# A four-layer graph network on one core: inputs and output by partition, adjacency loads in halves, the gates' matmuls spread by chunk

## The chip, the cores and the metric

The kernel runs on one core of one Trainium2 chip, in one launch. The metric is the device time of a run in microseconds (us); the figure quoted for a kernel is the median of its runs, and a ratio compares such times. A separate execution is recorded by the hardware profiler. It has its own time and a span, from its first to its last recorded instruction.

## What is computed

There are 32 independent batches. Each has a feature matrix `x` of 512 x 128 and a dense adjacency matrix `adj` of 512 x 512, all in float32. Four residual layers are applied one after the other, each to a row-normalized and rectified copy of the features:

```python
h = relu(layernorm(x)); x = x + gcn(h, adj)        # L0: normalized by the degree on both sides
h = relu(layernorm(x)); x = x + io_gnn(h, adj)     # L1: adj @ in, adj.T @ out, a node term, tanh
h = relu(layernorm(x)); x = x + unet(h, adj)       # L2: four inner layers with l2-normalized adj
h = relu(layernorm(x)); x = x + gru(h, adj)        # L3: message, then a gated recurrent unit
```

One inner layer of L2 computes `tanh(concat(src_agg, self, dst_agg) @ wu + bu)`, where `src_agg` uses the adjacency normalized along its rows and `dst_agg` the one normalized along its columns. The inner layers take 1, 1, 2 and 3 feature matrices as input, because earlier results are concatenated again. L3 forms `m = tanh(adj @ (h @ W + b))` and then the gates `r`, `z`, `n` from `m` and `h`; the result is `(1 - z) * n + z * h`.

## The kernel before

**Tiling.** The 512 rows of a batch are four chunks (`NC` = 4) of 128 partitions. A feature tile in rows is 128 x 4 x 128, an adjacency tile is 128 x 4 x 512 (1 MB). The kernel holds `adj` as `a` and its transpose as `aT`; `aT` is loaded a second time as `aT2` for L3, since `a` and `aT` are overwritten by their l2-normalized versions (line 602). Weights stay in SBUF; the products of the L2 weights that can be folded are folded once in `setup`. A float32 matmul is seen as two records on TensorE, with a weight load each.

**An operation list and a planner.** `program(b)` does not emit instructions. It records operations for one batch, with an engine, an estimated duration, the buffers read and written and a function that emits the instruction. `Plan.order` (lines 149 to 219) then plays the whole list with these estimates: each engine takes, whenever it is free, the ready operation with the smallest key. The key is a due time, `batch * PERIOD - tail`, where `tail` is the estimated length of the longest chain behind the operation in its batch. The result is one fixed order of instructions for every engine, across all batches. The engines then run these orders strictly in sequence and wait on semaphores. In this way some three batches are in flight at any time: a batch's L1 and its first L2 layers fill TensorE beside the later layers of the batch before it. The planner's durations are estimates (for instance `t_pow`, line 272, for GpSimd's power, and 240 GB/s plus 1.3 us for a DMA, line 99); real durations only shift waits, not the order.

**What a batch does**, with the names that the traces show:

- L0 (lines 498 to 538): `degree` reduces `a` on VectorE (line 503); GpSimd raises variance and degree to the power -0.5 (`sc`, line 404); ScalarE makes `h` from `x` in four instructions (line 416); GpSimd adds the identity to the diagonal blocks of `aT` (`diag`, line 514); TensorE aggregates into `ps_agg`, then `ps_lin`; VectorE makes `z`, `y` and the new features `xr`.
- L1 (lines 541 to 575): normalization again (`bn`, `mv`, `v`, `sc`, `nb`, `h`), a transposition `hT`, two banks of `ps_sd`, `rep`, two aggregations with `aT` and `a`, `ps_upd`, `u`, `y`, `xr`.
- L2 (lines 578 to 634): `inv` is 1/norm of rows and columns, sent through DRAM (`bounce`, `rows`) and multiplied into `aT` and `a` by eight VectorE instructions (line 602). Then, for each of four inner layers, `paired_rows` fills two banks `ps_sd`, VectorE adds a bias to each (`sd`, line 489), and eight matmuls of 512 columns aggregate into `ps_agg`; ScalarE takes the tanh (`f`, line 619). These results are called f1 to f4 below, the transposed input f0.
- L3 (lines 637 to 688): `msg`, the aggregation with `aT2`, `mT` (line 649), and for each of four chunks a bank `ps_gate` with four matmuls: two from `h3T` (128 and 256 columns) and two from `mT` (256 and 128 columns), lines 652 to 660. Then the gate arithmetic `g`, `u`, `q`, `w`, `n`, `xo`, and the store of `out`. For the last two batches (`at_end`) this arithmetic runs by chunk and partly on GpSimd, otherwise on whole tiles.

For the batches 3 to 29 a transposition goes through VectorE (32 x 32 blocks, `blk`, line 425), four DMAs of 64 KB to DRAM (line 434) and one DMA back (line 438); for the others through TensorE (`ps_t`).

**Order of transfers.** All loads and stores except two small ones are issued by SyncE (SP), in one queue order, also taken from the plan. An adjacency load is one DMA of 1 MB (line 378, and line 646 for `aT2`), except for batch 0, which is loaded in four pieces. A DMA that waits for its buffer to come free holds back everything behind it on SP.

The matmuls are all recorded by one helper (line 287):

```python
def mm(ps, out_of, lhs, rhs, n, start, stop, reads, part=None):
    op("PE", t_mm(n), lambda: nc.tensor.matmul(out_of(ps.ap()), lhs(), rhs(), start=start, stop=stop),
       reads, [(ps, part) if part is not None else ps])
```

Of the kernel before, what the change touches and what calls it, by code (L numbers as in the profile page):

```python
# [13 lines left out]
F32 = mybir.dt.float32  # L14
# [66 lines left out]


class Op:
    __slots__ = ("engine", "us", "land", "emit", "after", "next", "waits", "bufs", "batch", "rank", "tail", "ready", "key")


class Plan:
# [28 lines left out]
    def bank(self, name):  # L116
        return self.buf("bank", name=f"ps_{name}")

    def op(self, engine, us, emit, reads=(), writes=(), kb=0.0, rank=None):


        o = Op()
        o.engine, o.us, o.land, o.emit, o.batch, o.rank = engine, us, 0.0, emit, self.batch, rank
        if kb:
            o.us, o.land = max(us, kb / self.RATE), self.TRANSFER
        o.after, o.next, o.bufs = {}, [], []
        for group, written in ((reads, False), (writes, True)):
            for item in group:
                buf, part = item if isinstance(item, tuple) else (item, None)
                if written and buf.old is not None:  # L130
                    for other, _, _ in buf.old.uses:
                        o.after[other] = True
                for other, p, w in buf.uses:
                    if (w or written) and other is not o and (part is None or p is None or part & p):
                        o.after[other] = True
                buf.uses.append((o, part, written))
                if buf not in o.bufs:
                    o.bufs.append(buf)
        self.ops.append(o)
        return o  # L140
# [8 lines left out]
    def order(self):  # L149
        for i, o in enumerate(self.ops):  # L150
            o.waits, o.ready = len(o.after), 0.0
            for other in o.after:
                other.next.append(o)
            for buf in o.bufs:
                buf.left += 1
        for i, o in reversed(list(enumerate(self.ops))):
            o.tail = max([o.us + o.land] + [self.lag(o, n) + n.tail for n in o.next if n.batch == o.batch])

            due = o.batch * PERIOD if o.batch < B - 1 else (B - 2) * PERIOD + ENDING
            o.key = (due - o.tail if o.rank is None else o.rank - 1e6, i)  # L160
        free = {k: list(range(n)) for k, n in self.places.items()}
        unfinished = {}
        for o in self.ops:
            unfinished[o.batch] = unfinished.get(o.batch, 0) + 1
        queues, idle_at = {e: [] for e in self.SIGNAL}, dict.fromkeys(self.SIGNAL, 0.0)
        events, seq = [], 0

        def event(at, what, o=None):
            nonlocal seq
            seq += 1  # L170
            heapq.heappush(events, (at, seq, what, o))

        for o in self.ops:
            if not o.waits:
                event(0.0, "ready", o)
        done = []
        while events:
            now = events[0][0]
            while events and events[0][0] <= now + 1e-9:
                _, _, what, o = heapq.heappop(events)  # L180
                if what == "ready":
                    heapq.heappush(queues[o.engine], (o.key, o))
                elif what == "end":
                    for buf in o.bufs:
                        buf.left -= 1
                        if not buf.left and buf.kind in free:
                            free[buf.kind].append(buf.slot)
                    unfinished[o.batch] -= 1
                    if not unfinished[o.batch]:
                        del unfinished[o.batch]  # L190
            for e, queue in queues.items():
                if idle_at[e] > now + 1e-9:
                    continue
                held, o = [], None
                while queue and o is None:
                    item = heapq.heappop(queue)
                    new = [x for x in item[1].bufs if x.slot is None and x.kind in free]
                    older = item[1].batch - min(unfinished)
                    if any(len(free[x.kind]) < len([y for y in new if y.kind == x.kind]) + older * self.kept.get(x.kind, 0) for x in new):
                        held.append(item)  # L200
                        continue
                    o = item[1]
                    for x in new:
                        x.slot = free[x.kind].pop(0)
                for item in held:
                    heapq.heappush(queue, item)
                if o is None:
                    continue
                done.append(o)
                idle_at[e] = now + o.us  # L210
                event(now + o.us, "idle")
                event(now + o.us + o.land + self.SIGNAL[e], "end", o)
                for n in o.next:
                    n.waits -= 1
                    n.ready = max(n.ready, now + self.lag(o, n))
                    if not n.waits:
                        event(n.ready, "ready", n)
        assert len(done) == len(self.ops), "the plan does not end"
        return done
# [3 lines left out]
def gnn_stack(  # L223
# [60 lines left out]
        ("w1", w_sb), ("w2", w_sb), ("w3", w_sb), ("c_sb", c_sb), ("r_sb", r_sb), ("rf_sb", rf_sb),  # L284
        ("cf_sb", cf_sb), ("ident", ident), ("neg_half", neg_half)))

    def mm(ps, out_of, lhs, rhs, n, start, stop, reads, part=None):
        op("PE", t_mm(n), lambda: nc.tensor.matmul(out_of(ps.ap()), lhs(), rhs(), start=start, stop=stop),  # L288
           reads, [(ps, part) if part is not None else ps])

    def setup():

# [64 lines left out]
    def program(b):  # L357
# [10 lines left out]

        xt, a, aT = buf("s2", rows_shape, "x"), buf("s8", (P, NC, N), "a"), buf("s8", (P, NC, N), "aT")

        pieces = NC if b == 0 else 1

        def load(dst, src, kb, rank):

            n = NC // pieces
            for k in range(pieces):
                s = slice(k * n, (k + 1) * n)
                op("SP", 0.4, lambda s=s: nc.sync.dma_start(dst.ap()[:, s, :], src.rearrange("(c p) n -> p c n", p=P)[:, s, :]),
                   [], [(dst, set(range(NC)[s]))], kb=kb / pieces, rank=None if b else rank)

        op("SP", 0.4, lambda: nc.sync.dma_start(xt.ap(), x[b].rearrange("(c p) d -> p c d", p=P)), [], [xt], kb=256, rank=None if b else 0)
        load(a, adj[b], 1024, 1)
        load(aT, adjt[b], 1024, 4)

# [112 lines left out]

        def degree(v8):
            stat = buf("stat", (P, NC))
            n = NC // pieces  # L500
            for k in range(pieces):
                s = slice(k * n, (k + 1) * n)
                op("DVE", t_tt(n * N), lambda s=s: nc.vector.tensor_reduce(stat.ap()[:, s], a.ap()[:, s, :], AX.X, ALU.add),  # L503
                   [(a, set(range(NC)[s]))], [(stat, {k})])
            op("DVE", 0.08, lambda: nc.vector.tensor_scalar_add(v8.ap()[:, NC:], stat.ap(), 1.0), [stat], [(v8, {1})])
# [7 lines left out]
            blocks = bass.AP(tensor=t.tensor, offset=t.offset + k * (N + P), ap=[list(t.ap[0]), [N + P, n], [1, P]])  # L513
            nc.gpsimd.tensor_tensor(diag.ap()[:, k:k + n, :], blocks, ident[:, None, :].to_broadcast([P, n, P]), op=ALU.add)

        for k in range(0, NC, NC // pieces):
            n = NC // pieces
            op("POOL", t_pool(n * P), lambda k=k, n=n: own(k, n), [(aT, set(range(k, k + n))), ID], [(diag, set(range(k, k + n)))])
        psh = plan.bank("agg")
        for c in range(NC):  # L520
# [122 lines left out]
           N, [psm, (RS, {2})])  # L643
        psa = plan.bank("agg")
        aT2 = buf("s8", (P, NC, N), "aT2")
        op("SP", 0.4, lambda: nc.sync.dma_start(aT2.ap(), adjt[b].rearrange("(c p) n -> p c n", p=P)), [], [aT2], kb=1024)
        aggregate(psa, msg, 0, aT2)
        mT = buf("s2", name="mT")
        op("ACT", t_act(N), lambda: nc.scalar.activation(mT.ap(), psa.ap(), AF.Tanh), [psa], [mT])  # L649
# [2 lines left out]
        for c in range(NC):  # L652
            ps = plan.bank("gate")
            blk = slice(c * P, (c + 1) * P)
            for m, lo, n, col, start, stop in ((h3T, 3, 1, W_L3_HH + 2 * D, True, True), (h3T, 0, 2, W_L3_HH, True, False),
                                               (mT, 0, 2, W_L3_IH, False, True), (mT, 2, 1, W_L3_IH + 2 * D, True, True)):
                mm(ps, lambda t, lo=lo, n=n: t[:, lo * D:(lo + n) * D], lambda m=m, blk=blk: m.ap()[:, blk],
                   lambda col=col, n=n: wt(col, n * D), n * D, start, stop, [m, W3])
            op("DVE", t_tt(N), lambda ps=ps, c=c: nc.vector.tensor_add(g.ap()[:, c, :], ps.ap(), r_sb[:, R_L3_G:R_L3_G + 4 * D]),  # L659
               [ps, RS], [(g, {c})])  # L660

# [10 lines left out]
        for k in range(0, NC, w2):  # L672
            s, part, cols = slice(k, k + w2), set(range(k, k + w2)), w2 * D

            def step(dst, fn, reads, engine="DVE"):
# [8 lines left out]
            step(q, lambda s=s: side.tensor_tensor(q.ap()[:, s, :], q.ap()[:, s, :], x3.ap()[:, s, :], op=ALU.add), [q, x3], side_engine)  # L684
            step(n, lambda s=s: nc.vector.tensor_mul(n.ap()[:, s, :], n.ap()[:, s, :], w.ap()[:, s, :]), [n, w])
            step(xo, lambda s=s: nc.vector.tensor_add(xo.ap()[:, s, :], q.ap()[:, s, :], n.ap()[:, s, :]), [q, n])
            op("SP", 0.4, lambda s=s: nc.sync.dma_start(out[b].rearrange("(c p) d -> p c d", p=P)[:, s, :], xo.ap()[:, s, :]),
               [(xo, part)], [], kb=cols / 2)

    setup()  # L690
# [44 lines left out]
```

## Time and profile before

| quantity | value |
|---|---|
| median of 5 runs | 2386.19 us |
| lowest and highest run | 2384.91 and 2386.62 us |
| the profiled execution's own time | 2385.46 us |
| its span | 2383.5 us |
| TensorE matmul (PE) busy | 2337.3 us, 98% of the span |
| VectorE (DVE) busy | 1297.6 us, 54% |
| ScalarE (ACT) busy | 790.4 us, 33% |
| GpSimd (POOL) busy | 352.0 us, 15% |
| DMA, mean over the span | 82 GB/s |

How to read it: the profiled execution lies 0.73 us below the median of the runs, and 1.96 us of it are outside its span. A busy share is an average; for a chain of dependent work it says little. A timeline row gives the start in the span, the length, the engine, the line, the operation, what it writes and reads, and in brackets how long the engine had been idle before and what ended that. The DMA view gives, for each issue, its size and the time until it has landed. A queue name such as SPq is an engine's sequencer.

### The profile page before, as it was taken

The page shows a single profiled execution, that of the slowest core. Times are in us where ns is not written, and L with a number is a line of the kernel's source. Part 1 is how long each engine was busy: PE and PEld are TensorE (multiplying, and loading weights), DVE is VectorE, ACT ScalarE, POOL GpSimd, SP SyncE. Part 2 cuts the span into 40 slices and gives each one's busy share as a digit, 9 for nine tenths or more (in the row PEclk, how much of TensorE's full clock was granted, in tenths as well). Part 3 has the DMA queues.
Part 4 walks back from the last instruction along what each step waited for, and adds up shares of the span by engine and source line. Part 5 has one row for each costly group of instructions (what it writes and reads, how often), then busy time and mean ns, then how long its engine had stood idle before and what let it go on. Part 6 is the DMA issues. An engine that isn't in the chain of part 4 may idle for free.

```text
span 2383.5 us, 23873 instructions
## 1 busy us (share of the span) xinstructions
PE 2337.3 (98%) x8466; PEld 1427.7 (60%) x8466; DVE 1297.6 (54%) x2963; ACT 790.4 (33%) x1719; POOL 352.0 (15%) x218
## 2 busy tenths in 40 slices
PE   6999999999999999999999999999999999999998
PEld 4565566565666556665556665656655566656655
DVE  6445445565555665555665556654556654554623
ACT  5324223433323333233333234332233322343312
POOL 2101011111011111111110111111111111111001
PEclk9999999999999999999999999999999999999999
DMA  5212122332313222223223132322232232232000
GB/s 216 78 53 68 57 77 83 89 100 86 100 55 102 89 90 96 78 73 104 87 84 107 54 97 89 97 89 85 67 106 89 82 104 63 88 106 71 18 9 9
DMA packets 173206, 196.34 MB, mean 82 GB/s; under 512 B 16800, under 2 KB 105248, under 8 KB 173088
## 3 DMA queue, kind: packets, MB, share of 16 engines
q1 hardware_dynamic: 172800, 194.70, 25.8%
q8 instruction: 66, 1.08, 0.2%
q14 instruction: 52, 0.43, 0.1%
q10 hardware_dynamic: 288, 0.13, 0.0%
HBM read 157.95 MB, written 36.83 MB: 82 GB/s over the span
## 4 chain that ended last, share of the span: by engine, by line
PE 70%; DVE 13%; POOL 7%; ACT 3%; DMA 2%; issue 2%; SPq 1%; POOLq 0%; ACTq 0%; DVEq 0%
PE ps_agg L288 44%; PE ps_sd L288 16%; POOL sc L404 7%; PE ps_gate L288 6%; DVE aT L602 2%; ACT h L416 2%; DVE sd L489 2%; DVE bn L388 2%; DVE a L602 1%; DVE rep L558 1%; PE ps_msg L288 1%; PE ps_lin L288 1%; ACT f L619 1%; DVE node L551 1%; PE ps_upd L288 1%
## 5 line engine op out<-in xcount | busy, mean ns | idle before, releaser
L404 POOL TENSOR_TENSOR sc<-v,neg_half 128x4 f32<-128x4 f32 (+1 forms) x128 | 250.1, 1954 | 1963.6 <-DVE v L391 1908.5
L288 PE MATMUL ps_agg<-aT,sd 128*128 128x512 f32 x1024 | 512.2, 595 | 1.0 <-DVE sd L489 1.0
L288 PE MATMUL ps_agg<-a,sd 128*128 128x512 f32 x1024 | 496.9, 592 | 0.0
L288 PE MATMUL ps_sd<-w_sb,f 128*128 128x256 f32 x1792 | 482.2, 382 | 9.2 <-ACT f L619 8.5
L288 PEld LDWEIGHTS ps_sd<-w_sb,f 128*128 128x128 f32 x1792 | 333.2, 191 | 235.6 <-issue 198.0
L489 DVE TENSOR_TENSOR sd<-ps_sd,rf_sb 128x512 f32<-128x512 f32 x256 | 176.3, 689 | 359.6 <-PE ps_sd L288 357.1
L416 ACT ACTIVATE h<-xr,nb,sc 128x128 f32<-128x128 f32 x384 | 158.0, 482 | 482.9 <-DVE nb L412 482.9
L288 PEld LDWEIGHTS ps_agg<-a,sd 128*128 128x128 f32 x1024 | 185.6, 191 | 164.6 <-issue 155.3
L288 PEld LDWEIGHTS ps_agg<-aT,sd 128*128 128x128 f32 x1024 | 186.9, 190 | 129.0 <-issue 87.7
L288 PE MATMUL ps_agg<-f,w_sb 128*128 128x512 f32 x448 | 229.7, 594 | 0.0
L619 ACT ACTIVATE f<-ps_agg,cf_sb 128x512 f32<-128x512 f32 x128 | 87.2, 681 | 219.9 <-PE ps_agg L288 219.9
L503 DVE TENSOR_REDUCE stat<-a 128x4 f32<-128x2048 f32 (+1 forms) x35 | 73.5, 2102 | 141.0 <-DMA a<-in_adj 141.0
L602 DVE TENSOR_TENSOR a<-a,rows 128x512 f32<-128x512 f32 x128 | 138.5, 1085 | 3.8 <-PE ps_agg L288 3.8
L602 DVE TENSOR_TENSOR aT<-aT,rows 128x512 f32<-128x512 f32 x128 | 137.7, 1081 | 4.5 <-PE ps_agg L288 4.5
L288 PE MATMUL ps_agg<-aT,rep 128*128 128x512 f32 x256 | 130.9, 593 | 2.2 <-DVE rep L558 2.2
L288 PE MATMUL ps_agg<-a,rep 128*128 128x512 f32 x256 | 130.7, 592 | 0.0
L288 PE MATMUL ps_agg<-aT,msg 128*128 128x512 f32 x256 | 125.6, 592 | 0.0
L288 PE MATMUL ps_agg<-aT,h 128*128 128x256 f32 (+2 forms) x384 | 109.9, 383 | 0.0
L412 DVE SCALAR_TENSOR_TENSOR nb<-mv,sc 128x4 f32<-128x4 f32 x128 | 50.8, 397 | 95.4 <-POOL sc L404 95.0
L642 DVE TENSOR_TENSOR msg<-ps_msg,r_sb 128x512 f32<-128x512 f32 x32 | 22.1, 690 | 146.7 <-PE ps_msg L288 146.7
L659 DVE TENSOR_TENSOR g<-ps_gate,r_sb 128x512 f32<-128x512 f32 x128 | 79.5, 683 | 32.1 <-PE ps_agg L288 20.9
L288 PE MATMUL ps_gate<-w_sb,mT 128*128 128x128 f32 (+1 forms) x512 | 94.3, 327 | 0.4 <-ACT mT L649 0.4
(99 smaller groups left out, 2698.5 us busy)
## 6 DMA issues: line engine op xcount, KB each, us to landing
aT<-in_adjt SPq DMA_DIRECT2D x63, 1024.0 KB, 5.6
a<-in_adj SPq DMA_DIRECT2D x31, 1024.0 KB, 5.6
turn_turned<-blk SPq DMA_DIRECT2D x324, 64.0 KB, 1.8
turned<-turn_turned SPq DMA_DIRECT2D x81, 256.0 KB, 2.6
rows<-bounce SPq DMA_DIRECT2D x32, 512.0 KB, 3.8
x<-in_x SPq DMA_DIRECT2D x32, 256.0 KB, 3.0
out<-xo SPq DMA_DIRECT2D x30, 256.0 KB, 2.4
turn_f4r<-blk SPq DMA_DIRECT2D x108, 64.0 KB, 1.9
```

What stands on the lines that cost most here:

```text
L288: op("PE", t_mm(n), lambda: nc.tensor.matmul(out_of(ps.ap()), lhs(), rhs(), start=start, stop=stop), reads, [(ps, part) if part is not Non ...
L388: op("DVE", 0.193, lambda c=c: nc.vector.bn_stats(st.ap()[:, c, :], xin.ap()[:, c, :]), [xin], [(st, {c})])
L404: op("POOL", t_pow(n), lambda: nc.gpsimd.tensor_tensor(inv.ap()[:, :n], v8.ap()[:, :n], neg_half[:, :n], op=ALU.pow), [v8, NH], [(inv, {0})])
L412: op("DVE", 0.08, lambda: nc.vector.scalar_tensor_tensor(nb.ap(), mv.ap()[:, :, 0], -1.0, inv.ap()[:, at:at + NC], op0=ALU.mult, op1=ALU.m ...
L416: op("ACT", t_act(D, 2), lambda c=c: nc.scalar.activation(h.ap()[:, c, :], xin.ap()[:, c, :], AF.Relu, bias=nb.ap()[:, c:c + 1], scale=inv ...
L489: op("DVE", t_tt(N), lambda ps=ps, h=h: nc.vector.tensor_add(sd.ap()[:, 2 * h:2 * h + 2, :], ps.ap().rearrange("p (j v) -> p j v", j=2), a ...
L503: op("DVE", t_tt(n * N), lambda s=s: nc.vector.tensor_reduce(stat.ap()[:, s], a.ap()[:, s, :], AX.X, ALU.add), [(a, set(range(NC)[s]))], [ ...
L551: tt(node, lambda: nc.vector.tensor_max(node.ap(), zn.ap(), en.ap()), N, [zn, en])
L558: op("DVE", t_tt(N), lambda s=s: nc.vector.tensor_max(rep.ap()[:, s, :], rep.ap()[:, s, :], io.ap()[:, s, :]), [(rep, part), (io, part)], ...
L602: op("DVE", 1.0, lambda m=m, c=c, s=s: nc.vector.tensor_mul(m.ap()[:, c, :].rearrange("p (k n) -> p k n", k=NC), m.ap()[:, c, :].rearrange ...
L619: op("ACT", t_act(N, 1), lambda ps=ps, i=i, f_new=f_new: nc.scalar.activation(f_new.ap(), ps.ap(), AF.Tanh, bias=cf_sb[:, i:i + 1]), [ps, ...
L659: op("DVE", t_tt(N), lambda ps=ps, c=c: nc.vector.tensor_add(g.ap()[:, c, :], ps.ap(), r_sb[:, R_L3_G:R_L3_G + 4 * D]), [ps, RS], [(g, {c})])
```

## The change

Four edits, apart from a parameter that is taken out (`part` of `mm`, which no call used).

1. **Layout by partition.** On the host, `x`, `adj` and its transpose are rearranged from rows `(c p)` to `p, c`, and the output is rearranged back. A partition's four chunks are then contiguous in DRAM: a row of a 1 MB adjacency load is one run of 8 KB per partition where it was four runs of 2 KB, and `x` one of 2 KB where it was four of 512 B.
2. **Halves.** For every batch but the first, `a`, `aT` and `aT2` are loaded by two DMAs of 512 KB, two chunks each. (`aT2` of batch 0 becomes four DMAs.) Both halves are separate operations for the planner. `degree` and `own` keep their sizes: one instruction for all four chunks in batches 1 to 31.
3. **Gates.** An operation can have a `later` time, which is added to its key. The gate matmuls of chunk `c` get `0.7 * c`.
4. Since the planner orders everything by key and by its own clock, edits 2 and 3 also move instructions that they do not name, on all engines.

```diff
-    def op(self, engine, us, emit, reads=(), writes=(), kb=0.0, rank=None):
+    def op(self, engine, us, emit, reads=(), writes=(), kb=0.0, rank=None, later=0.0):
...
-            o.key = (due - o.tail if o.rank is None else o.rank - 1e6, i)
+            o.key = (due - o.tail + o.later if o.rank is None else o.rank - 1e6, i)
...
-        pieces = NC if b == 0 else 1
+        pieces = NC if b == 0 else 2
...
-                op("SP", 0.4, lambda s=s: nc.sync.dma_start(dst.ap()[:, s, :], src.rearrange("(c p) n -> p c n", p=P)[:, s, :]),
+                op("SP", 0.4, lambda s=s: nc.sync.dma_start(dst.ap()[:, s, :], src[:, s, :]),
                    [], [(dst, set(range(NC)[s]))], kb=kb / pieces, rank=None if b else rank)
...
-        op("SP", 0.4, lambda: nc.sync.dma_start(xt.ap(), x[b].rearrange("(c p) d -> p c d", p=P)), [], [xt], kb=256, rank=None if b else 0)
+        op("SP", 0.4, lambda: nc.sync.dma_start(xt.ap(), x[b]), [], [xt], kb=256, rank=None if b else 0)
...
-            n = NC // pieces
-            for k in range(pieces):
+            n = NC if b else 1
+            for k in range(NC // n):
...
-        op("SP", 0.4, lambda: nc.sync.dma_start(aT2.ap(), adjt[b].rearrange("(c p) n -> p c n", p=P)), [], [aT2], kb=1024)
+        load(aT2, adjt[b], 1024, None)
...
-                   lambda col=col, n=n: wt(col, n * D), n * D, start, stop, [m, W3])
+                   lambda col=col, n=n: wt(col, n * D), n * D, start, stop, [m, W3], later=0.7 * c)
...
-            op("SP", 0.4, lambda s=s: nc.sync.dma_start(out[b].rearrange("(c p) d -> p c d", p=P)[:, s, :], xo.ap()[:, s, :]),
+            op("SP", 0.4, lambda s=s: nc.sync.dma_start(out[b][:, s, :], xo.ap()[:, s, :]),
...
+    def by_partition(m):
+
+        return np.ascontiguousarray(m.reshape(B, NC, P, -1).transpose(0, 2, 1, 3))
...
-        "x": np.ascontiguousarray(g["x"]),
-        "adj": np.ascontiguousarray(g["adj"]),
-        "adjt": np.ascontiguousarray(g["adj"].transpose(0, 2, 1)),
+        "x": by_partition(g["x"]),
+        "adj": by_partition(g["adj"]),
+        "adjt": by_partition(g["adj"].transpose(0, 2, 1)),
...
-    args.append(nc.dram_tensor("out", (B, N, D), F32, kind="ExternalOutput").ap())
+    args.append(nc.dram_tensor("out", (B, P, NC, D), F32, kind="ExternalOutput").ap())
```

More of the change, by code (lines that the diff above doesn't have):

```diff
@@ L83 @@
 class Op:
-    __slots__ = ("engine", "us", "land", "emit", "after", "next", "waits", "bufs", "batch", "rank", "tail", "ready", "key")
+    __slots__ = ("engine", "us", "land", "emit", "after", "next", "waits", "bufs", "batch", "rank", "later", "tail", "ready", "key")
 class Plan:
@@ L117, in bank @@
         return self.buf("bank", name=f"ps_{name}")
-    def op(self, engine, us, emit, reads=(), writes=(), kb=0.0, rank=None):
+    def op(self, engine, us, emit, reads=(), writes=(), kb=0.0, rank=None, later=0.0):
         o = Op()
-        o.engine, o.us, o.land, o.emit, o.batch, o.rank = engine, us, 0.0, emit, self.batch, rank
+        o.engine, o.us, o.land, o.emit, o.batch, o.rank, o.later = engine, us, 0.0, emit, self.batch, rank, later
         if kb:
@@ L285, in gnn_stack, with mm @@
         ("cf_sb", cf_sb), ("ident", ident), ("neg_half", neg_half)))
-    def mm(ps, out_of, lhs, rhs, n, start, stop, reads, part=None):
+    def mm(ps, out_of, lhs, rhs, n, start, stop, reads, later=0.0):
         op("PE", t_mm(n), lambda: nc.tensor.matmul(out_of(ps.ap()), lhs(), rhs(), start=start, stop=stop),
-           reads, [(ps, part) if part is not None else ps])
+           reads, [ps], later=later)
     def setup():
@@ L514, in own @@
             nc.gpsimd.tensor_tensor(diag.ap()[:, k:k + n, :], blocks, ident[:, None, :].to_broadcast([P, n, P]), op=ALU.add)
-        for k in range(0, NC, NC // pieces):
-            n = NC // pieces
+        n = NC if b else 1
+        for k in range(0, NC, n):
             op("POOL", t_pool(n * P), lambda k=k, n=n: own(k, n), [(aT, set(range(k, k + n))), ID], [(diag, set(range(k, k + n)))])
@@ L733 @@
     r = run_bass_kernel_spmd(nc, [{f"in_{k}": v for k, v in arrays.items()}], core_ids=[0])
-    return r.results[0]["out"]
+    return np.ascontiguousarray(r.results[0]["out"].transpose(0, 2, 1, 3)).reshape(B, N, D)
```

## The prediction

> **What bounds the kernel now.** I read the page's busy shares first, then the chain of work that ended last, the stretches, and the timelines of one period, of the head and of the tail.
>
> ```profile
> PE 2337.3 (98%) x8466; PEld 1427.7 (60%) x8466; DVE 1297.6 (54%) x2963; ACT 790.4 (33%) x1719; POOL 352.0 (15%) x218
> ...
> PE 70%; DVE 13%; POOL 7%; ACT 3%; DMA 2%; issue 2%; SPq 1%; POOLq 0%; ACTq 0%; DVEq 0%
> ```
>
> TensorE is busy for 98%, and the change leaves every matmul in place (4276, with the same columns). So it can gain or lose only where TensorE waits. The stretches show the head:
>
> ```profile
> 0.00:20.00 20.00, 9.32 (x46) 8.34 (x47) 6.25 (x21) 8.74 (x21) 4.23 (x12) 1.00 0.87 322
> 20.00:40.00 20.00, 15.02 (x73) 10.72 (x73) 16.40 (x47) 8.64 (x22) 4.37 (x4) 0.91 0.90 322
> 40.00:60.00 20.00, 12.94 (x64) 8.44 (x62) 18.77 (x47) 14.33 (x40) 6.90 (x6) 0.86 0.01 1
> ```
>
> 22.7 of the first 60 us are idle PE. From 100 us on PE is full, and batches follow every 72.5 us. Within that period the timeline shows one clear wait:
>
> ```profile
> 1028.10 2.72 POOL L404 TENSOR_TENSOR sc<-v,neg_half 128x4 f32<-128x4 f32 x1 [4.47 <-DVE v L391]
> 1028.85 1.09 DVE L602 TENSOR_TENSOR a<-a,rows 128x512 f32<-128x512 f32 x1
> ...
> 1030.85 0.16 DVE L412 SCALAR_TENSOR_TENSOR nb<-mv,sc 128x4 f32<-128x4 f32 x1 [0.91 <-POOL sc L404]
> ...
> 1031.05 1.65 ACT L416 ACTIVATE h<-xr,nb,sc 128x128 f32<-128x128 f32 x4 [1.55 <-DVE nb L412]
> ...
> 1032.58 0.39 PE L288 MATMUL ps_upd<-w_sb,agg_out 128*128 128x128 f32 x2
> 1032.61 0.67 ACT L619 ACTIVATE f<-ps_agg,cf_sb 128x512 f32<-128x512 f32 x1
> ...
> 1033.32 0.92 PE L288 MATMUL ps_sd<-w_sb,f 128*128 128x256 f32 x3 [0.35 <-ACT f L619]
> ```
>
> PE has only 1.34 us of other work (six `ps_upd` matmuls of 0.223) between the end of f2's aggregation and the first matmul that reads f2. ScalarE makes four `h` for L3 first, late because `nb` waited for GpSimd. That `sc` takes 2.72 us where the same form elsewhere takes 1.01: it ends 0.87 after VectorE's multiplications (L602) end. The two records at 1032.58 are 0.11 apart, so PE was due at 1032.80: a gap of **0.52**, and 0.1 more because the first record after a gap takes 0.32 instead of 0.215. Sum 0.63. Gaps of this kind recur 23 times, from 380 to 1977 us.
>
> A smaller wait hides inside a busy row, in f3's second `ps_sd` bank:
>
> ```profile
> 1069.16 1.01 POOL L404 TENSOR_TENSOR sc<-v,neg_half 128x4 f32<-128x4 f32 x1 [30.62 <-DVE v L391]
> ...
> 1070.14 1.27 POOL L514 TENSOR_TENSOR diag<-aT,ident 128x512 f32<-128x512 f32 x1
> ...
> 1070.20 1.23 DVE L412 SCALAR_TENSOR_TENSOR nb<-mv,sc 128x4 f32<-128x4 f32 x1 [1.19 <-POOL sc L404]
> ...
> 1071.47 2.93 PE L288 MATMUL ps_agg<-aT,sd 128*128 128x512 f32 x6
> 1071.67 0.69 DVE L489 TENSOR_TENSOR sd<-ps_sd,rf_sb 128x512 f32<-128x512 f32 x1 [0.24 <-PE ps_sd L288]
> ```
>
> The next group starts at 1074.24, 2.77 later; six records of 0.43 are 2.58, so **0.19** is a wait for `sd`, with one matmul as cover. The lines also show `nb` at 1.23 instead of 0.16 while `diag` runs on GpSimd.
>
> **Part by part.** Durations are of the profiled execution, 2385.46 us (span 2383.5 and 1.96 around it), 0.73 below the median of the runs shown.
>
> *Layout and halves.* 96 more DMAs on SyncE, 0.4 us of issue each, three per period of 72.5 us, while SyncE mostly waits: nothing on the path. The load of `a` is issued at 1055.67 and lands 5.5 us later; VectorE waits 5.72 for it, reduces until 1063.51 and needs that result only behind later work. By the new order some 5 us of slack stand between the reduction and the point E0 below. Bounds: a landing up to 2 us earlier (half the bytes, where nothing waits) and up to twice the present 5.5 both cost nothing or, at the far end, about 0.5 per period. I take 0, nearest to the load's own row. On SyncE, `bounce` and `rows` now come before the turns of L3's `h` and `turned`; `ps_msg`, 13 us later on PE, is their only user, with some 6 us spare. `f4r` goes between the halves of `aT2`, and lands earlier.
>
> (The Trainium skill, "DMA: Bandwidth & Descriptors", section "Measured", asks for at least 1 MiB per DMA; its fit of 2.0 us plus bytes over 436 GB/s would be an estimated 3.2 us per half, and 6.4 if two ran in series. The trace has 5.6 for the whole MB in 2 KB runs. With 6.4 the sum below would not change, since 0.9 fits in the slack.)
>
> *Gates and order, per period.* By the changed order of PE, the gates' matmuls now lie singly between f3's banks and f1's aggregation. Behind the second f3 bank (its end is **E0**) 1.5 us of other matmuls and more stand before its reader, where there was 0.86. So the 0.19 goes. But VectorE's `v` of L1's normalization now stands behind the `sd` of that bank, and all VectorE work until L3's `nb` follows in one row. From E0, by start-to-start distances of rows in the trace:
>
> - 0.20 to `sd` (1071.47 to 1071.67), 0.61 `sd`; `v` to `blk`, `diag` collision included, 4.35 (1068.85 to 1073.20); `blk` 0.64; `g` until the second tanh, 3.19 (1074.44 to 1077.63): 8.99.
> - u, u 1.25; q, q 1.2; n 0.68; `sd` 0.6; xo 0.6; `blk` 0.64; L1's two `sd` 1.2: 15.16.
> - `rep` with one `sd` 2.65; three L602 3.0; `bn`, `mv` of the next x 1.06; L602 1.0: 22.87.
> - `v`, then `sc` of eight columns on GpSimd: 0.33 to its start, 1.6 of its own, 2.35 standing still while VectorE's L602, `en`, `xr`, `node` run, in all 4.3 (3.95 if `en` does not hold it): 27.17. Add 0.08 and L602 1.0: 28.25.
> - `v`, two L602, `sc` ending 0.87 behind them, `nb`: `h` starts 3.31 later. **Three** `h` (the fourth now stands behind f2) 1.17, f2 0.71: 33.4.
>
> On PE the new order has between E0 and the end of f2's aggregation 30 matmuls of 512 columns, 9 of 256 and 7 of 128: 30 x 0.858 + 9 x 0.43 + 7 x 0.223 = 31.2; with the 1.34 behind it PE wants f2 at 32.55. The gap becomes 0.87 + 0.1 = 0.97 instead of 0.63: +0.34 - 0.19 = **+0.15 per period**, times 23 = **+3.5**. Bounds: without a gap -0.82 (-18.9); with VectorE 0.5 later than summed +0.65 (+15).
>
> Other margins in the new order: L1's `hT` (E0 + 12.3 against 12.67) and f1 (about 0.4). They hold, but barely.
>
> *Head.* `nb` of batch 0 takes 1.21 at 26.72 because `diag` of batch 1 runs beside it, and `ps_t` starts behind it. In the new order `aT` of batch 1 comes later on SyncE, so that collision goes: -1.05. VectorE idles 1.76 at 41.2 for `sc`; multiplications now fill part of it, some 0.8, ahead of
>
> ```profile
> 57.71 1.63 PE L452 MATMUL ps_t<-ident,h 128*128 128x128 f32 x4 [5.33 <-ACT h L416]
> ```
>
> In all **-1.85** (bounds -3, the two whole, and +0.5, if `diag` holds another row).
>
> *Tail.* In the timeline of the last 15 us:
>
> ```profile
> 2370.16 0.58 ACT L649 ACTIVATE mT<-ps_agg 128x512 f32<-128x512 f32 x1
> ...
> 2370.79 2.88 PE L288 MATMUL ps_gate<-w_sb,mT 128*128 128x256 f32 x16 [0.44 <-ACT mT L649]
> 2373.04 2.48 DVE L659 TENSOR_TENSOR g<-ps_gate,r_sb 128x512 f32<-128x512 f32 x4 [1.72 <-PE ps_gate L288]
> ```
>
> PE does four 256-column and one 128-column matmuls before the first `g`, 1.93; by chunk it needs one of each, 0.65: -1.3. `mT` also leaves ScalarE's queue about 1.0 earlier. The four chunks no longer come in one burst, which I price at +0.7. Sum **-1.6** (bounds -2.9 and +0.9, every chunk waiting).
>
> *Sum.* 2385.46 + 3.5 - 1.85 - 1.6 = **2385.5**. About 0.2% is what a measurement of this kernel can tell from no change: 2381.4 to 2391.0.
>
> **Rivals.**
>
> 1. *The gap at f2 vanishes.* VectorE's row is 0.9 shorter than summed, for example because `diag` no longer falls on `nb` (1.07). For: `diag` collides only by 0.1 us of timing. Against: GpSimd's order is unchanged, `diag` directly behind `sc`. Then -0.82 x 23: 2385.46 - 18.9 - 3.45 = 2363; half of it, 2373.
> 2. *The turn of L1's `h` comes late* (slower). `blk` ends at E0 + 5.9; four DMAs, one back and the copy take 6.4 (1073.91 to 1080.32), against 12.67 on PE. Beyond the margin of 0.35 each 0.1 costs 2.3 us, since PE and VectorE's `sd` both wait; it decides from about 0.6 late (2391). For: `f4r`, the same turn beside a 1 MB load, took 5.5 instead of 2.6. Against: no load is due in that stretch. One `sd` (0.6) and 0.4 of issue late gives 0.65 x 23: 2400.
> 3. *The ends bring nothing*: 2389.
>
> **How the numbers follow.** Forecast 0.45 (2379 to 2392), rival 1 0.22 (2362 to 2376), rival 2 0.23 (2393 to 2410), rival 3 0.10 (2386 to 2392). Faster: 0.22 and a fifth of the forecast, 0.31. Slower: 0.23, 0.04 of the forecast's upper edge, 0.03 of rival 3: 0.30. Same: 0.39. The range 2368 to 2400 leaves out about half of each of rivals 1 and 2.
>
> **What would show it.** Per period: a gap before `ps_sd<-w_sb,f` near 0.9 behind three `h`, none behind f3's second bank, `nb` still 1.23. Periods near 72.65 us. A wait for `hT` speaks for rival 2, no wait for f2 for rival 1. Head: `ps_t` near 55.9. Tail: first `g` about 2.3 before its old distance from the last aggregation. The forecast is wrong if VectorE meets a wait in that row that I have not seen, or PE's waits lie elsewhere.

## The result

The changed kernel takes 2390.87 us in the median of 28 runs (2389.09 to 2393.19). The kernel before, in 48 runs beside them, takes 2386.09. The ratio is 1.002, with a 95% interval of 1.0015 to 1.0025: 0.2% slower, where 2385.5 and next to no change was forecast. The time lies in the stated range, but the change is clear of the noise.

**The profile after.** Three parts of the page: the span, the busy shares and the chain that ended last.

```profile
span 2388.2 us, 23862 instructions
...
PE 2330.0 (98%) x8466; PEld 1430.2 (60%) x8466; DVE 1286.1 (54%) x2963; ACT 792.4 (33%) x1719; POOL 355.8 (15%) x218
...
PE 65%; DVE 21%; POOL 7%; ACT 3%; issue 1%; DMA 1%; SPq 0%; ACTq 0%; DVEq 0%; POOLq 0%
```

PE does the same 8466 records, in a span that is 4.7 us longer. In the chain PE has fallen from 70 to 65% and DVE has risen from 13 to 21%: more of the end hangs on VectorE. What PE waits for stands in its waits view (us in total, times, longest). First before, then after:

```profile
PE ps_t L452 <- ACT h L416: 9.0, 3, 5.3
PE ps_sd L288 <- ACT f L619: 8.5, 24, 0.4
```

```profile
PE ps_sd L289 <- ACT f L620: 24.7, 24, 1.3
...
PE ps_t L453 <- ACT h L417: 7.0, 3, 3.8
```

The head has lost 2 us of waiting for `h`; the wait for f2 has grown from 8.5 to 24.7 us over the same 24 places. The start of `mT` (L3's tanh on ScalarE), one per batch, cuts the run into parts:

| part | before | after | difference | forecast |
|---|---|---|---|---|
| start to `mT` of batch 3 | 402.8 | 402.1 | -0.7 | -1.85 |
| 23 periods, batch 3 to 26 | 1668.7 | 1677.0 | +8.3 | +3.5 |
| `mT` of batch 26 to the end of the span | 312.0 | 309.0 | -3.0 | -1.6 |
| span | 2383.5 | 2388.2 | +4.7 | |

Nearly all periods last 72.5 us before and 73.03 after; three of the 23 after last only 72.05. The forecast of the ends is off by +1.2 and -1.4, which nearly cancel; the miss is in the periods.

One period after, in the timeline of its engines (start, length, engine, line, what it writes and reads; in brackets the idle time before it and what ended that):

```profile
1073.51 0.69 DVE L490 TENSOR_TENSOR sd<-ps_sd,rf_sb 128x512 f32<-128x512 f32 x1 [4.81 <-PE ps_sd L289]
1074.12 0.16 DVE L392 TENSOR_SCALAR v<-mv 128x4 f32<-128x4 f32 x1
1075.40 1.22 DVE L413 SCALAR_TENSOR_TENSOR nb<-mv,sc 128x4 f32<-128x4 f32 x1 [1.12 <-POOL sc L405]
1078.34 0.71 DVE L426 STREAM_TRANSPOSE blk<-h 128x512 f32<-128x512 f32 x1 [1.71 <-ACT h L417]
1079.32 2.48 DVE L660 TENSOR_TENSOR g<-ps_gate,r_sb 128x512 f32<-128x512 f32 x4 [0.27 <-PE ps_agg L289]
1082.50 0.69 DVE L679 SCALAR_TENSOR_TENSOR u<-g 128x512 f32<-128x512 f32 x1 [0.70 <-ACT g L670]
```

```profile
1102.04 2.08 DVE L603 TENSOR_TENSOR a<-a,rows 128x512 f32<-128x512 f32 x2
1105.04 0.16 DVE L413 SCALAR_TENSOR_TENSOR nb<-mv,sc 128x4 f32<-128x4 f32 x1 [0.91 <-POOL sc L405]
```

```profile
1102.14 2.86 POOL L405 TENSOR_TENSOR sc<-v,neg_half 128x4 f32<-128x4 f32 x1 [1.36 <-DVE nb L413]
```

```profile
1105.23 1.26 ACT L417 ACTIVATE h<-xr,nb,sc 128x128 f32<-128x128 f32 x3 [1.42 <-DVE nb L413]
1106.40 0.67 ACT L620 ACTIVATE f<-ps_agg,cf_sb 128x512 f32<-128x512 f32 x1
```

```profile
1105.64 0.39 PE L289 MATMUL ps_upd<-w_sb,agg_out 128*128 128x128 f32 x2
1107.12 1.56 PE L289 MATMUL ps_sd<-w_sb,f 128*128 128x256 f32 x6 [1.09 <-ACT f L620]
```

This is the picture that was forecast: `v` behind f3's second `sd`, `nb` at 1.22 beside `diag`, `sc` standing still beside the multiplications, three `h`, then f2. PE's two records at 1105.64 end its other work at 1105.86, which is E0 (1073.31) + 32.55, as computed. Only f2 comes later than forecast: PE starts at 1107.12, E0 + 33.81 instead of 33.4. The gap is **1.26**, not 0.87.

### The profile page after: what moved, and what is told of

Its sections match the earlier page's. It is cut to its first block, busy times and chain, and to the rows that moved or that the text cites. A ratio compares the mean times of both kernels' runs of the same rounds, so it can differ in the third digit from the quotient of the medians.

```text
span 2388.2 us, 23862 instructions
## 1 busy us (share of the span) xinstructions
PE 2330.0 (98%) x8466; PEld 1430.2 (60%) x8466; DVE 1286.1 (54%) x2963; ACT 792.4 (33%) x1719; POOL 355.8 (15%) x218
## 3 DMA queue, kind: packets, MB, share of 16 engines
q8 instruction: 66, 1.08, 0.2%
## 4 chain that ended last, share of the span: by engine, by line
PE 65%; DVE 21%; POOL 7%; ACT 3%; issue 1%; DMA 1%; SPq 0%; ACTq 0%; DVEq 0%; POOLq 0%
PE ps_agg L289 40%; PE ps_sd L289 15%; POOL sc L405 7%; PE ps_gate L289 6%; DVE aT L603 3%; DVE g L660 3%; DVE a L603 3%; DVE sd L490 2%; DVE rep L559 1%; ACT h L417 1%; PE ps_msg L289 1%; DVE bn L389 1%; PE ps_lin L289 1%; DVE u L679 1%; DVE u L680 1%
## 5 line engine op out<-in xcount | busy, mean ns | idle before, releaser
L289 PE MATMUL ps_agg<-aT,sd 128*128 128x512 f32 x1024 | 520.9, 593 | 0.4 <-DVE sd L490 0.4
L289 PE MATMUL ps_sd<-w_sb,f 128*128 128x256 f32 x1792 | 487.0, 382 | 25.7 <-ACT f L620 24.7
L289 PEld LDWEIGHTS ps_sd<-w_sb,f 128*128 128x128 f32 x1792 | 327.0, 191 | 201.1 <-issue 132.5
L289 PEld LDWEIGHTS ps_gate<-w_sb,mT 128*128 128x128 f32 x512 | 95.3, 190 | 61.6 <-issue 55.0
L289 PE MATMUL ps_gate<-w_sb,mT 128*128 128x256 f32 (+1 forms) x512 | 123.1, 326 | 0.0
L289 PEld LDWEIGHTS ps_gate<-w_sb,hT 128*128 128x128 f32 x512 | 91.0, 190 | 49.8 <-issue 43.5
L426 DVE STREAM_TRANSPOSE blk<-h 128x512 f32<-128x512 f32 x81 | 57.6, 711 | 116.4 <-ACT h L417 116.4
L289 PE MATMUL ps_gate<-w_sb,hT 128*128 128x128 f32 (+1 forms) x512 | 119.0, 327 | 0.0
```

The lines of the kernel that those rows point to most:

```text
L426: op("DVE", t_tt(N), lambda: nc.vector.transpose(blk.ap().rearrange("p b (c r) -> p c b r", c=NC), m.ap().rearrange("p c (b s) -> p c b s" ...
```

## The experiments

The theory at first: whatever stands ahead of f2 on ScalarE, at the end of a VectorE row (instructions that follow one another with next to no idle time) that begins at E0, the end of f3's second bank, sets the period. The rivals: the transfers cost the time; the spread gates cost it; the row is anchored elsewhere. Ratios are to the kernel before on the same chip, with 95% intervals.

**f2 first.** The planner is told that L3's `sc` takes 1.2 us longer. The work is the same, but the four `h` of L3 fall behind f2.

```diff
-            op("POOL", t_pow(n), lambda: nc.gpsimd.tensor_tensor(inv.ap()[:, :n], ...
+            op("POOL", t_pow(n) + slow, lambda: nc.gpsimd.tensor_tensor(inv.ap()[:, :n], ...
...
-        def normed(xin, out_tag, extra=None):
+        def normed(xin, out_tag, extra=None, slow=0.0):
...
-        h3, _ = normed(x3, "h")
+        h3, _ = normed(x3, "h", slow=1.2)
```

> The changed kernel, except that the planner takes L3's sc on GpSimd for 1.2 us longer (2.5 for 1.3); the chip's work is the same, but f2 now stands ahead of L3's four h on ScalarE. Theory: the gap of 1.26 us goes in nearly every period, period 71.7 to 71.9: 2362 to 2367 us. Rival (VectorE's whole row is late, and f2 is only where it shows): another wait takes its place, on L1's hT or on u or sd, period over 72.5, 2382 or more.

Measured: 2368.85 us, ratio 0.9929 (0.9912 to 0.9946). The period is 72.0. The wait for f2 has gone from the periods; what is left is the next one in the row. Two of the rows of PE's waits:

```profile
PE ps_sd L289 <- ACT hT L458: 2.0, 8, 0.4
PE ps_sd L289 <- ACT f L620: 0.9, 3, 0.5
```

By start-to-start distances the wait for L1's `hT` stands in all 23 periods, 0.11 to 0.54 long and 0.28 in the mean (a record's modelled end hides part of it in the view). So the gap at f2 was the loss, and the margin at `hT`, rival 2 of the prediction, is real: it is used up once the gap no longer gives the turn (the transposition through DRAM) time. The 2 to 7 us by which the time exceeds the expectation are this wait; the last run below takes it away.

**Layout and halves, gates not delayed.** `later=0.7 * c` becomes `later=0.0 * c` in the changed kernel.

> The changed kernel without the delay of the gate matmuls: layout and halves. The new order makes L3's h early, but puts the copy hT of L3 directly ahead of f2 on ScalarE. Theory: the period is decided by that copy, so by the landing of the turn: between 71.8 (no gap) and 72.8 us, 2368 to 2391 us, and the trace shows the gap ahead of f2 ended by hT's DMA if there is one. Rival (the halves' 96 more DMAs cost the time of the changed kernel): period 73.0, about 2391, with the gap unlike that of before.

Measured: 2396.89 us, ratio 1.0045 (1.003 to 1.006). Neither account hit: the gap before f2 is gone, the 0.19 in f3 is back, and PE waits elsewhere.

```profile
PE ps_upd L289 <- ACT agg_in L564: 12.1, 20, 1.3
```

In this order one `h` of L0 of the next batch stands ahead of the copy `agg_in` on ScalarE, and waits for its own `nb`. It is the same kind of wait at another place; the expectation went only through the instructions ahead of f2, and so missed it.

**Layout alone.** The kernel before with the host's rearrangement and the DMAs' new sources; `pieces` stays 1.

```diff
-                ... dst.ap()[:, s, :], src.rearrange("(c p) n -> p c n", p=P)[:, s, :] ...
+                ... dst.ap()[:, s, :], src[:, s, :] ...
```

> The kernel before with the layout by partition alone: every engine's order of instructions is the one of before, only the DMAs' runs are longer. Theory (what stands ahead of f2 on ScalarE and VectorE sets the period): the period stays 72.5 us, the gap ahead of f2 0.52; only the head, where the DMA engines are 0.87 to 0.90 busy, can gain, up to 1.5 us: 2384 to 2387 us. Rival (the transfers themselves slow the changed kernel): the period grows, 2389 or more.

Measured: 2386.72 us, ratio 0.9997 (0.9988 to 1.0006), period 72.5: no difference in the time. The loads did become faster. The DMA view, first before, then this run:

```profile
a<-in_adj SPq DMA_DIRECT2D x31, 1024.0 KB, 5.6
```

```profile
a<-in_adj SPq DMA_DIRECT2D x31, 1024.0 KB, 4.8
```

A load of `a` lands 0.8 us earlier in the median, and nothing on the path waited for it. The head gained nothing: DMA moves 330 GB/s at a share of 0.90 in the first 20 us, where it was 322 at 0.87.

**Layout and delayed gates, loads whole.** The run before this one plus edit 3.

> Layout and the gates' delay, adjacency loads whole: in this order f2 stands ahead of all four h of L3 on ScalarE, and the spread gates and VectorE's row from E0 are those of the changed kernel. Theory: f2 is ready in time, its gap goes, and what is left is the wait for L1's hT of about 0.3 that the run with f2 first shows: period near 72.0 us, 2366 to 2371 us. Rival (the spread gates themselves cost TensorE time, whatever stands ahead of f2): period 73.0, about 2391.

Measured: 2366.53 us, ratio 0.9912 (0.9897 to 0.9926). The period is 71.66, against 71.58 of matmuls alone (52 of 512 columns, 2 of 384, 42 of 256 and 34 of 128, by 0.8583, 0.645, 0.4305 and 0.223 us from the trace's distances). The spread gates cost TensorE nothing. The wait for L1's `hT` that was expected to remain is not there; why was not tried. With halves and the same gates it is 2390.87: the difference of 24 us is made by the order that the planner finds when each load is two operations, and the f2-first run shows that it is the order and not the transfers, since it has all the halves and takes 2368.85.

**diag in four.** In the changed kernel GpSimd's `diag` becomes four instructions of one chunk, so that `nb` waits less.

```diff
-        n = NC if b else 1
+        n = 1
         for k in range(0, NC, n):
```

> The changed kernel with diag in four GpSimd instructions of one chunk for every batch, as batch 0 has it; all other orders stay, three h of L3 still stand ahead of f2. Theory (f2 is late by the length of VectorE's row from E0): nb waits for one chunk of diag (0.45) instead of 1.22, the row is 0.75 shorter, the gap ahead of f2 falls from 1.26 to about 0.5, period 72.3, about 2375 us. Rival (the gap is set behind the row, by GpSimd's sc between the last multiplications and h alone, at a time that TensorE gives): period still 73.0, about 2391.

Measured: 2391.62 us, ratio 1.0017 (1.0007 to 1.0027), period 73.03. **The theory failed here.** The row did become shorter where it should, and nothing came of it. (In the head, within the first 460 of TensorE's 8466 records, the engines' orders differ from those of the changed kernel; from there on they are the same.)

```profile
1076.80 0.69 DVE L490 TENSOR_TENSOR sd<-ps_sd,rf_sb 128x512 f32<-128x512 f32 x1 [4.80 <-PE ps_sd L289]
...
1078.69 0.41 DVE L413 SCALAR_TENSOR_TENSOR nb<-mv,sc 128x4 f32<-128x4 f32 x1 [1.12 <-POOL sc L405]
1080.81 0.71 DVE L426 STREAM_TRANSPOSE blk<-h 128x512 f32<-128x512 f32 x1 [1.72 <-ACT h L417]
1082.60 2.48 DVE L660 TENSOR_TENSOR g<-ps_gate,r_sb 128x512 f32<-128x512 f32 x4 [1.08 <-PE ps_agg L289]
```

`blk` starts 4.01 behind `sd` instead of 4.83, but `g` starts 5.80 behind it, where it was 5.81. The idle time ahead of `g` grew from 0.27 to 1.08, and it is ended by PE, by a `ps_agg` matmul that `g` does not read. So the row is anchored at `g`, not at E0: the rival hit the number, but the place is another. The plan tells by what: `g` (8 KB per partition, kind `s8`, ten slots) takes its slot in the moment when `aT` of the next batch is given up, and the last reader of that `aT` is the fourth matmul of f3's `sd` with it. In the changed kernel that matmul starts at 1078.26 and the next one follows at 1079.12:

```profile
1078.26 1.02 PE L289 MATMUL ps_agg<-aT,sd 128*128 128x512 f32 x2
1079.12 1.45 PE L289 MATMUL ps_agg<-a,sd 128*128 128x512 f32 x3
```

`g` starts 0.20 later, at 1079.32. Before, the four `aT` matmuls ran one behind the other and were through at 1074.24, and `g` started again 0.20 later:

```profile
1074.44 2.49 DVE L659 TENSOR_TENSOR g<-ps_gate,r_sb 128x512 f32<-128x512 f32 x4 [0.52 <-PE ps_agg L288]
```

The release has moved from 2.8 to 5.8 us behind the end of f3's second bank. It is the gates' delay that moves it: without it (layout and halves) these distances are 2.77 again, and with it and whole loads 5.80.

**g in memory of its own.** The changed kernel, every engine's order the same. To find 8 KB, the small statistics rotate over 8 copies instead of 16.

```diff
-SMALL = 16
+SMALL = 8
...
-            ... tag=f"{self.kind}_{self.slot}" ...
+            ... tag="own_g" if self.name.startswith("g_") else f"{self.kind}_{self.slot}" ...
```

> The changed kernel with g in memory of its own (8 KB per partition, gained by 8 instead of 16 copies of the small statistics); the orders of all engines are exactly the same. Theory (VectorE's row starts with g, and g waits until the fourth aT matmul of f3's aggregation gives up the slot of aT): g starts behind blk instead, 0.25 earlier, the gap ahead of f2 is 1.0 instead of 1.26, about 2386 us. Rival (g waits for something else on TensorE): g starts 6.0 us behind the end of f3's second bank as before, 2391.

Measured: 2376.35 us, ratio 0.996 (0.9945 to 0.9975), period 72.31 in every batch. The anchor is confirmed: the wait ahead of `g` is gone in all periods, and the traces show the same order of instructions on every engine.

```profile
1070.35 0.69 DVE L490 TENSOR_TENSOR sd<-ps_sd,rf_sb 128x512 f32<-128x512 f32 x1 [4.80 <-PE ps_sd L289]
...
1075.24 0.71 DVE L426 STREAM_TRANSPOSE blk<-h 128x512 f32<-128x512 f32 x1 [1.71 <-ACT h L417]
1075.88 2.44 DVE L660 TENSOR_TENSOR g<-ps_gate,r_sb 128x512 f32<-128x512 f32 x4
```

The gain, 14.5 us, is three times the expected one: the anchor was right, the size was luck. A shift of 0.28 at `g` is 0.16 at `v` of the next x (22.90 behind `sd`, where it was 23.06). It has become 0.72 at L3's `nb`, because GpSimd's `sc` of eight columns, which starts between the two, now takes 2.40 where it took 3.96, and `sc<-sc` no longer waits 0.48. Why `sc` takes its shorter length here is not shown:

```profile
1093.55 2.40 POOL L405 TENSOR_TENSOR sc<-v,neg_half 128x8 f32<-128x8 f32 x1 [20.04 <-DVE v L392]
```

**g in its own memory and diag in four.**

> The run with diag in four, and g in memory of its own; same orders. Theory: with the slot out of the way the earlier nb counts, the row is 1.0 us shorter, the gap ahead of f2 about 0.25, period 72.0, about 2369 us. Rival (the row does not decide): 2386 to 2391 us.

Measured: 2375.94 us, ratio 0.9957 (0.9943 to 0.9971), period 72.31 again. `g` now starts 4.71 behind `sd`, as it should, but the row meets a third anchor before f2. The first multiplication of `aT` idles for TensorE:

```profile
1088.17 1.09 DVE L603 TENSOR_TENSOR aT<-aT,rows 128x512 f32<-128x512 f32 x1 [0.15 <-PE ps_agg L289]
```

It overwrites a chunk that L1's aggregation still reads, and starts 17.84 behind `sd` in both runs. From there on the two runs are alike. The expectation had counted the row as continuous behind `g`.

**sc left out.** In the changed kernel, L3's normalization leaves out the power -0.5: VectorE copies `v` to `sc`.

```diff
-            ... nc.gpsimd.tensor_tensor(inv.ap()[:, :n], v8.ap()[:, :n], neg_half[:, :n], op=ALU.pow) ...
+            ... nc.vector.tensor_scalar_add(inv.ap()[:, :n], v8.ap()[:, :n], 0.0) ...   # in L3 alone
```

> The changed kernel, but L3's normalization leaves out the power: VectorE copies v to sc (tensor_scalar, +0.0) in place of GpSimd's instruction; all else in the same order. The copy stands between the last two multiplications. Theory (behind g the row is continuous up to f2, and GpSimd's sc stands still while VectorE multiplies): h starts 0.9 earlier, the gap ahead of f2 is about 0.35, period 72.1, about 2372 us. Rival (h waits for something other than sc): no change, 2391.

Measured: 2368.64 us, ratio 0.9929 (0.9914 to 0.9944), period 72.11, and a gap of 0.34 ahead of f2 by start-to-start distances. The end of the row, from `sc` through `h` to f2, is the path; one GpSimd instruction of four columns is worth 0.9 us per period there.

**f2 first and diag in four**, the two edits together.

> The run with f2 first, and diag in four. Theory: what is left there is L1's hT, 0.28 late per period because its h waits for nb behind diag; with nb 0.75 earlier that wait goes too: period 71.7, 2360 to 2364 us, below both kernels. Rival (hT is late by its DMAs, not by nb): period 72.0, 2369 us.

Measured: 2360.59 us, ratio 0.9888 (0.9873 to 0.9902), period 71.65. It is the fastest version, 1.1% below the kernel before. With f2 out of the row, `nb` does count, because L1's `hT` is next: the wait for it is gone. ScalarE makes f2 at 1092.62 and starts the four `h` of L3 at 1093.21.

## Why the prediction was wrong

*The place was right.* The gap ahead of f2, the three `h`, `nb` beside `diag` and the order of VectorE were as read from the new order. f3's 0.19 went, as forecast: 71.58 of matmuls, the gap of 1.26 and 0.1 behind it, and 0.1 of other small waits give the 73.03, and nothing is left for it.

*The step that failed is the sum of VectorE's row,* "33.4" from E0, and with it "+0.15 per period". The row took 33.81, so the gap is 1.26 and not 0.87. (The bound given, "VectorE 0.5 later than summed", holds it.) In blocks, forecast and measured:

| from - to | forecast | measured |
|---|---|---|
| E0 - first `u` | 8.99 | 9.19 |
| first `u` - first `rep` | 6.17 | 6.44 |
| `rep` - `v` of the next x | 7.71 | 7.63 |
| to L3's `v` | 5.38 | 5.33 |
| to PE's start | 5.15 | 5.22 |

The first block has the unseen wait of `g` for `aT`'s slot: from `blk` to `g` the row took 0.98 where the sum had 0.64, and `v` to `blk` gave back 0.13 (4.22 for 4.35). The wait was visible in the profile of before, in the row at 1074.44 above: `g` had idled 0.52 until a `ps_agg` matmul of PE, a releaser that the instruction does not read. The sum took `g` to follow `blk` at once, and the row to begin at E0; the run with `diag` in four, which made the stretch ahead of `g` shorter by 0.82 and gained nothing, shows that it begins at `g`.

The second block has pairs. Where one VectorE instruction reads what the one before it wrote (`u`, `u` and `q`, `q`), they start 0.72 apart; the independent ones in the same rows start 0.60 to 0.61 apart. The sum took both pairs from the trace of before, where they were interleaved. The pairs make 0.21 of the 0.27, `n` is 0.07 shorter, and 0.15 stands between L1's two `sd` and the first `rep`, which waits for ScalarE's exponential of the first of them (1.35 for 1.2).

With the 0.41 that the row is longer, the forecast of +0.15 becomes +0.56 per period; measured is 73.03 - 72.52 = +0.51. Twenty periods at that make 10, and three short ones give 1.4 back (0.47 each); a few irregular periods of before, from 71.84 to 73.55, make the rest of the way to 8.3. The row was forecast to about 1%, but the gap is the small difference of two long sums, and 0.2 us per period are already 0.2% of the time.

*The three short periods* were not forecast either. In them L3's `sc` takes 1.86 instead of 2.87:

```profile
593.86 1.86 POOL L405 TENSOR_TENSOR sc<-v,neg_half 128x4 f32<-128x4 f32 x1 [1.36 <-DVE nb L413]
```

Its length alone is 1.01, so it stood still for about one of VectorE's two multiplications instead of both. What decides between the two was not found: VectorE's instructions around it start at the same distances, to 0.02 us, as in long periods.

*Layout and halves at nothing*: right as to the transfers. The reduction of `a` starts 5.33 us behind the first issue, where it was 5.55; with the layout alone, in the same period, it is 4.85. So the layout gave 0.7, the changed kernel with its halves took 0.5 back, and neither was on the path. (The prediction estimated 3.2 us for a half, and 6.4 for two in series, by a fit in the Trainium skill, "DMA: Bandwidth & Descriptors", section "Anatomy of one DMA — SWDGE (gpsimd) path". That fit is for DMAs issued from GpSimd; for these, issued from SyncE, the trace shows neither: the median of a half is 4.6 to 4.7, beside its other half.) But what the halves cost through the planner's order was not separated from the gates. The experiments do: without halves 2366.53, with them 2390.87.

*Head.* `nb` of batch 0 is 0.16, `diag` of batch 1 comes later, and `ps_t` of the second head gap starts at 54.22, 3.49 earlier, more than forecast:

```profile
54.22 1.63 PE L453 MATMUL ps_t<-ident,h 128*128 128x128 f32 x4 [3.78 <-ACT h L417]
```

By `mT` of batch 3 only 0.7 is left; batches 0 to 2 give back the rest in their own waits. Which of them does it was not tried.

*Tail.* From the last `mT` to the first `g` behind it the trace now has 1.59 (2375.31 to 2376.90) where it had 2.88: the 1.3 of the forecast. From the last-but-one `mT` to the end it is -2.5, and -0.5 in the four periods ahead, where -1.6 was forecast in all. How the rest divides between the earlier `mT` and the alternation of chunks was not tried.

*Rivals.* The example given for rival 1, `nb` free of `diag`, was tried with `diag` in four: `nb` took 0.41, and the gap stayed. Rival 2 was the right sign for another reason; `hT` has no wait in the changed kernel. The third anchor of the run with both edits, the multiplication that waits for L1's aggregation, was in none of the cases.

*A count.* The prediction has 4276 matmuls; the 8466 records are 4193 matmuls of two records and 80 transpositions of one, 4273. Nothing rests on it.

## What to carry to other kernels

When an instruction waits for an engine whose result it does not read, look at the buffer that it writes: here it waited for a slot, and the slot's last reader was the true start of its row. In a kernel that is full on one engine, list for each gap the instructions that stand ahead of the late one on its own engine; here it was cheaper to let f2 pass (1.1% with `diag` in four) than to shorten the row, which met a new anchor each time. A gap forecast as the difference of two long sums needs both ends in the range.

## What the runs showed of the hardware

- GpSimd's small instructions stand still beside VectorE's multiplications of two SBUF tensors, and not always for as long. `sc` of four columns took 1.01 alone, and 2.86 or 1.86 beside the same two multiplications of 1.0 in one kernel. The same form with eight columns took 1.64 alone, 3.96 in the changed kernel and 2.40 with `g` in memory of its own, beside the same VectorE instructions, at distances that differ by less than 0.1. The Trainium skill, "SBUF — State Buffer", section "SBUF: two separate sides", says that a VectorE instruction with two SBUF inputs and a GpSimd instruction that reads SBUF take a shared pair of ports by an exclusive lock, and hold it for the whole instruction. That four columns wait for one or both multiplications agrees. That VectorE is held in turn for a whole `sc` is not what these rows show: the last 0.95 of the `sc` of 1.86 lie beside the second multiplication, and the pair takes 2.10, where it takes 2.08 beside the `sc` of 2.86.
- The collision can work the other way too: `nb`, 0.16 alone, took 1.22 beside a `diag` of 1.26 and 0.41 beside one of 0.46.
- Longer runs in DRAM (8 KB instead of 2 KB) made a 1 MB load of `a` land in 4.8 us instead of 5.6 in the median, and changed nothing in the kernel's time: 0.9997.
